# One ring of four PSUM bank pairs in place of three pairs and two single banks

## The chip, the cores and the metric

The kernel runs on one core of one Trainium2 chip. The metric is the device time of one execution in microseconds (us), the median of several executions. Five engines work side by side, each through its own list of instructions in order: TensorE (PE in the profile; its weight loads are PEld), VectorE (DVE), ScalarE (ACT), GpSimd (POOL) and SyncE (SP), which mainly starts DMA transfers. Matmuls write to PSUM; here it is used as eight banks of 512 fp32 values in each of 128 partitions. DVE and ACT read the results out of it, which is called evacuation below.

## The reference

The input `x` is 4 sequences of 1024 tokens with 256 channels. The program is two residual layers, both fp32:

```python
x = x + attention(layernorm(x))     # 16 heads of 16, causal, ALiBi bias, softmax, output projection
x = x + encoder(layernorm(x))
```

The encoder layer takes the *batch* axis (4 long) as its sequence: at each of the 1024 positions, the four tokens attend to each other with 16 heads. Its output is added and normalised to `h`. A router scores 8 experts for each token, and the larger index of the best two is taken. That expert computes `gelu(h @ w1.T + b1) @ w2.T + b2`; the result is added to `h` and normalised again.

## The kernel before

`fast_layer` computes everything; a second, general version stands behind a test at the end and does not run on these inputs.

**Attention.** A unit is 256 queries of one sequence (128 in the last quarter, for which two units per sequence are made). For each unit and each of four groups of four heads, a round takes up to 512 columns of keys times queries. `score` (L902) makes a round's scores for four heads in two tiles `sk` of two banks each; ACT turns each tile into `p` with one exponential (L910) that reads both banks at once; where the diagonal is crossed, POOL cuts it (L920). `weigh` (L950) multiplies two rounds' `p` with the values into one bank `pv`, and ACT copies it (L966) or DVE adds it (L968) to `yt`. The results go through DRAM to be arranged by channel, are divided by their sums (L1010), projected (L1022, tile `op`), and added to `x` by DVE (L1015).

**What stands between.** While attention runs, the layer norm, transposes and projections of later units (`xtp` L806, `qkp` L820, `vp` L841) and the first six of eight encoder fronts are worked in between the rounds. A front is 128 positions of all four sequences: norm, transposes (`utp`, L1512), projections to queries, keys and values (`qkvp`, L1533, evacuated by ACT at L1542 and by DVE at L1540), attention over the batch on DVE, transposes (`ctp`), output projection (`ao`, L1640, added into `u` by DVE at L1645), routing. A loop over pairs of rounds, `p`, writes down the order: scores of round `2p`, work for DVE and ACT (`E_slot`), work that uses TensorE (`D_slot`), scores of round `2p + 1`, and the weighted sums of the two rounds before. `E_slot` and `D_slot` fill up to fixed costs. The order is written out by hand, so no scheduler changes it; the program builder adds the waits between engines from who reads and writes each tile.

**Banks.** A pool hands out its tiles in turn: a new tile takes the place of the one that the pool handed out `bufs` tiles ago, and its first writer waits until the readers of that one are done. Before, scores have a pool `ps_s` of three tiles of two banks. Everything else that TensorE writes in this stage takes one bank from `ps_m`, which has two, through `bank`:

```python
def bank(name):
    n_banks[0] += 1
    return banks[n_banks[0] % len(banks)].tile([P, QC], F32, tag="m", name=name)
```

`banks` is `[ps_m, ps_m]`. When attention is over, a third bank, `ps_z`, joins the turn.

**Experts.** After attention come the last unit's projection, the last two fronts and 38 tiles of 128 tokens, gathered by expert (`mtp` L1790, `hid` L1806, `oe` L1825, results by L1852 to L1863). They have a pool of five banks of their own beside the three of `bank`.

Of the kernel before, what the change touches and what calls it, by code (L numbers as in the profile page):

```python
# [29 lines left out]
F32 = mybir.dt.float32  # L30
# [5 lines left out]
PSUM = bass.MemoryType.PSUM  # L36

P = 128
# [6 lines left out]
QC = 512  # L45
# [529 lines left out]
def fast_layer(ctx: ExitStack, tc: tile.TileContext, odd, x, wq, wk, wv, wp, w_in, w_out, w_r,  # L575
# [5 lines left out]
    pool = lambda name, bufs, **k: tc.tile_pool(name=name, bufs=bufs, **k)  # L581
# [3 lines left out]
    xpool = ctx.enter_context(pool("xpool", X_BUFS))  # L585
    fact = ctx.enter_context(pool("fact", 1))
    ends = ctx.enter_context(pool("ends", 1))
    ps_m = ctx.enter_context(pool("ps_m", 2, space=PSUM))
    ctx.enter_context(tc.manual_schedule())
    attention = ExitStack()  # L590
    pad = attention.enter_context(pool("pad", 1))
    act = attention.enter_context(pool("act", 1))
    probs = attention.enter_context(pool("probs", N_PROBS))
    ps_s = attention.enter_context(pool("ps_s", 3, space=PSUM))

    def const(name, shape, dtype=F32, into=keep):
        return into.tile(shape, dtype, tag=name, name=name)
# [4 lines left out]
        return t  # L602


    banks, n_banks = [ps_m, ps_m], [0]

    def bank(name):
        n_banks[0] += 1
        return banks[n_banks[0] % len(banks)].tile([P, QC], F32, tag="m", name=name)

    batches = [(c, b) for c in range(NC) for b in range(B)]

# [187 lines left out]
    def turn(n):  # L800
        xn = held.pop(("xn", n))
        xt = act.tile([P, CC, W], F32, tag="xt", name=f"xt_{n}", bufs=2)
        pm = bank(f"xtp_{n}")
        for cc in range(CC):
            for i in range(PC):
                nc.tensor.transpose(  # L806
                    pm[:, cc * W + i * P:cc * W + (i + 1) * P],
                    xn[:, i, cc * P:(cc + 1) * P], ident,
                )
        nc.scalar.copy(xt.rearrange("p c w -> p (c w)"), pm)  # L810
        held["xt", n] = xt

    def project_qk(n, half):

        c, b = batches[n]
        xt = held["xt", n]
        pm = bank(f"qkp_{n}_{half}")
        for k in range(2):
            for cc in range(CC):
                nc.tensor.matmul(  # L820
                    pm[:, k * W:(k + 1) * W], wqk[:, k, cc, half * P:(half + 1) * P],
                    xt[:, cc], start=cc == 0, stop=cc == CC - 1,
                )
        kq = act.tile([P, 2, W], F32, tag=f"kq{half}", name=f"kq_{n}_{half}", bufs=KQ_BUFS)
        nc.vector.tensor_copy(kq.rearrange("p k w -> p (k w)"), pm)  # L825
        rows_ = slice(half * P, (half + 1) * P)
        if c == 0:
            held["kq", n, half] = kq
            nc.sync.dma_start(k_of[b][rows_, :2 * W], kq.rearrange("p k w -> p (k w)"))
        else:  # L830
            own = k_of[b][rows_, :W]
            both = bass.AP(own.tensor, own.offset, [own.ap[0], ((c + 1) * W, 2), (1, W)])
            nc.sync.dma_start(both, kq)
# [41 lines left out]
    def blocks_of(u, r):  # L875

        n, i, size = units[u]
        first = batches[n][0] * PC + i
        some = QC // (size * P)
        return [  # L880
            (kb, max(0, kb - first) * P)
            for kb in range(some * r, min(some * (r + 1), first + size))
        ]

    def n_rounds(u):
        n, i, size = units[u]
        return -(-(batches[n][0] * PC + i + size) // (QC // (size * P)))

    def score(u, g, r):

        n, i, size = units[u]
        name = f"{u}_{g}_{r}"
        kt = slots[g][:, W:]
        qt = slots[g][:, i * P:(i + size) * P]
        own = r == n_rounds(u) - 1
        ps = [ps_s.tile([P, 2, QC], F32, tag="s", name=f"sk_{name}_{k}") for k in range(2)]
        width = 0
        for kb, off in blocks_of(u, r):
            to = width + size * P - off
            for h in range(4):  # L900
                rows_ = slice(h * S, (h + 1) * S)
                nc.tensor.matmul(  # L902
                    ps[h // 2][:, h % 2, width:to],
                    kt[rows_, kb * P:(kb + 1) * P], qt[rows_, off:], start=True, stop=True,
                )
            width = to
        pts = []
        for pair in range(2):
            pt = probs.tile([P, 2, QC], F32, tag="p", name=f"p_{name}_{pair}")
            nc.scalar.activation(  # L910
                pt[:, :, :width], ps[pair][:, :, :width], AF.Exp, scale=1.0 / math.sqrt(D)
            )
            pts.append(pt)
        if own:

            for pt in pts:
                blocks = pt.rearrange("p j (n q) -> p j n q", q=W)[:, :, :, 0:P]
                if size == 1:
                    blocks = pt[:, :, width - P:width].unsqueeze(2)
                nc.gpsimd.affine_select(  # L920
                    blocks, blocks, pattern=[[0, 2], [0, size], [1, P]],
                    compare_op=ALU.is_ge, fill=0.0, base=0, channel_multiplier=-1,
                )
        return pts

    def weigh(rounds_):

        parts = []  # L930
        for u, g, r, pts in rounds_:
            if not parts or parts[-1][0] != (u, g):
                parts.append(((u, g), []))
            parts[-1][1].append((r, pts))
        pm = bank("pv_{}_{}_{}".format(*rounds_[0][:3]))
        for k, ((u, g), of_part) in enumerate(parts):
            n, i, size = units[u]
            c, b = batches[n]
            vt = values[b % 2]
            pv = pm[:, k * W:k * W + size * P]  # L940
            blocks = [
                (kb, off, pts, first) for r, pts in of_part
                for first, (kb, off) in zip((True, False, False, False), blocks_of(u, r))
            ]
            for m, (kb, off, pts, first) in enumerate(blocks):
                at_p = 0 if first else at_p
                to = at_p + size * P - off
                for h in range(4):
                    at = (4 * g + h) * VD
                    nc.tensor.matmul(  # L950
                        pv[h * S:(h + 1) * S, off:], vt[:, kb, at:at + S],
                        pts[h // 2][:, h % 2, at_p:to],
                        start=m == 0, stop=m == len(blocks) - 1,
                    )
                at_p = to
        for k, ((u, g), of_part) in enumerate(parts):
            n, i, size = units[u]
            c = batches[n][0]
            pv = pm[:, k * W:k * W + size * P]
            if of_part[0][0] == 0 and g % 2 == 0:  # L960
                held["yt", g // 2] = ends.tile(
                    [P, 2, W], F32, tag="yt", name=f"yt_{u}_{g}", bufs=2
                )
            yt = held["yt", g // 2][:, :, :size * P]
            if of_part[0][0] == 0:
                nc.scalar.copy(yt[:, g % 2], pv)  # L966
            else:
                nc.vector.tensor_tensor(yt[:, g % 2], yt[:, g % 2], pv, ALU.add)  # L968
            if g % 2 and of_part[-1][0] == n_rounds(u) - 1:
                (nc.sync if c else nc.scalar).dma_start(  # L970
                    y_of[u][g - 1:g + 1].rearrange("g p w -> p g w"), yt
                )
# [1129 lines left out]
    def score_next(k):  # L2102
        u, g, r = rounds[k]
        waiting.append((u, g, r, score(u, g, r)))
        if r == n_rounds(u) - 1 and u < last_unit:
            to_fill.append((u + 1, g))
# [5 lines left out]
    for p in range(len(rounds) // 2):  # L2112
# [12 lines left out]
        fill()  # L2125
        E_slot(2 * p + 1, then)
    weigh(waiting)
    attention.close()


    for p in range(len(rounds) // 2, len(rounds) // 2 + 3):
# [11 lines left out]
    tail = ctx.enter_context(pool("tail", 1))  # L2143
    work = ctx.enter_context(pool("work", 2))
    ps_x = ctx.enter_context(pool("ps_x", 1, space=PSUM))
    banks.append(ctx.enter_context(pool("ps_z", 1, space=PSUM)))

    w1_sb, w2_sb = (const(name, [P, E - 1, CC, C], into=tail) for name in ("w1", "w2"))

# [50 lines left out]
    def begin(it):  # L2200
        if it.kind == "DQ" and ("qkv",) in held or it.kind[1:] == "C" and part.placed < NT - 1:
            return 1e9
        return max(it.ready, free[engine_of[it.kind[0]]])
# [26 lines left out]
    while threads:  # L2230
# [4 lines left out]
        at, _, it = min((begin(it) + FIRST_BY * n, n, it) for n, it in enumerate(threads))  # L2235
# [15 lines left out]
    while experts.left():  # L2251
# [4 lines left out]
        if n == 11:  # L2256
            pm = bank("n_badp")
# [4 lines left out]
@with_exitstack  # L2262
def tile_layer(ctx: ExitStack, tc: tile.TileContext, *args):
    nc = tc.nc
    flag = ctx.enter_context(tc.tile_pool(name="flag", bufs=1))
    odd = flag.tile([P, 1], I32, tag="odd", name="odd")
    fast_layer(tc, odd, *args)
    again = nc.values_load(
        odd[0:1, 0:1], min_val=0, max_val=1,
        skip_runtime_bounds_check_because="a comparison's result",  # L2270
    )
    with tc.If(again > 0):
        general_layer(tc, *args)
# [75 lines left out]
```

## Time and profile before

| | before |
|---|---|
| median of 3 executions | 857.03 us (854.6 to 857.36) |
| the profiled execution | 867.75 us |
| its span in the profile | 866.0 us |
| mean granted TensorE clock | 0.942 |
| busy: PE / PEld / DVE / ACT / POOL | 733.2 / 540.0 / 547.1 / 418.1 / 253.5 us |

The profile shows one execution, and a little slower one than the median; durations below are from it. A view of groups or of the timeline gives for each the engine, the line, what is written and read, and in square brackets how long the engine stood idle before it and what released it. A view of waits gives who waited for whom, the total, how often, and the longest. Busy time of PE is modelled at the ends of matmuls, which overlap. Line numbers in the text are those of the kernel before.

### The profile page before, as it was taken

The page shows a single profiled execution, that of the slowest core. Times are in us where ns is not written, and L with a number is a line of the kernel's source. Part 1 is how long each engine was busy: PE and PEld are TensorE (multiplying, and loading weights), DVE is VectorE, ACT ScalarE, POOL GpSimd, SP SyncE. Part 2 cuts the span into 40 slices and gives each one's busy share as a digit, 9 for nine tenths or more (in the row PEclk, how much of TensorE's full clock was granted, in tenths as well). Part 3 has the DMA queues.
Part 4 walks back from the last instruction along what each step waited for, and adds up shares of the span by engine and source line. Part 5 has one row for each costly group of instructions (what it writes and reads, how often), then busy time and mean ns, then how long its engine had stood idle before and what let it go on. Part 6 is the DMA issues. An engine that isn't in the chain of part 4 may idle for free. (4 is left out here: it accounts for less than half of the span.)

```text
span 866.0 us, 22430 instructions
## 1 busy us (share of the span) xinstructions
PE 733.2 (85%) x8917; PEld 540.0 (62%) x8917; DVE 547.1 (63%) x1316; ACT 418.1 (48%) x625; POOL 253.5 (29%) x360
## 2 busy tenths in 40 slices
PE   3898779998899789989989898897997699777892
PEld 2665557666565466655567666576776468666672
DVE  7245226429546947693678638469579669885663
ACT  1454436655455645564455447356655145333440
POOL 5443113212111312111122112022111323648875
PEclk9799979999999999999989999899998789998997
DMA  7345344433522414252444435235521572233430
GB/s 205 105 136 154 114 133 133 140 106 114 162 73 69 129 49 154 62 149 65 112 128 124 135 105 153 62 96 160 148 75 27 159 262 64 67 115 117 127 91 24
DMA packets 75219, 99.54 MB, mean 115 GB/s; under 512 B 19497, under 2 KB 58724, under 8 KB 74597
## 3 DMA queue, kind: packets, MB, share of 16 engines
q1 hardware_dynamic: 64576, 79.63, 31.3%
q0 software_dynamic: 4864, 14.16, 5.6%
q10 hardware_dynamic: 5668, 4.25, 1.6%
q8 instruction: 72, 1.18, 0.6%
q14 instruction: 39, 0.31, 0.1%
HBM read 61.55 MB, written 35.12 MB: 112 GB/s over the span
## 5 line engine op out<-in xcount | busy, mean ns | idle before, releaser
L910 ACT ACTIVATE p<-sk 128x1024 f32<-128x1024 f32 (+1 forms) x320 | 289.8, 938 | 183.5 <-PE sk L902 157.1
L920 POOL TENSOR_SCALAR_AFFINE_SELECT p<-p 128x512 f32<-128x512 f32 (+1 forms) x160 | 104.8, 659 | 476.7 <-ACT p L910 474.7
L902 PE MATMUL sk<-slots 32*128 32x128 f32 (+1 forms) x3456 | 188.5, 333 | 21.8 <-ACT p L910 13.6
L902 PEld LDWEIGHTS sk<-slots 32*128 32x128 f32 x3456 | 140.2, 192 | 71.5 <-issue 41.6
L950 PE MATMUL pv<-p,v 128*32 128x128 f32 (+1 forms) x3456 | 145.1, 316 | 9.6 <-DVE yn L1053 3.6
L950 PEld LDWEIGHTS pv<-p,v 128*32 128x32 f32 x3456 | 97.1, 112 | 47.0 <-issue 8.5
L1533 PE MATMUL qkvp<-w_in,ut 128*128 128x264 f32 (+1 forms) x256 | 99.1, 522 | 7.6 <-DVE x L1015 3.0
L1533 PEld LDWEIGHTS qkvp<-w_in,ut 128*128 128x128 f32 x256 | 45.9, 199 | 43.6 <-issue 26.4
L820 PE MATMUL qkp<-xt,wqk 128*128 128x256 f32 x256 | 66.4, 405 | 2.2 <-ACT xt L810 2.2
L1540 DVE COPY qkv<-qkvp 128x264 f32<-128x264 f32 x28 | 12.1, 433 | 77.5 <-PE qkvp L1533 77.5
L820 PEld LDWEIGHTS qkp<-xt,wqk 128*128 128x128 f32 x256 | 50.2, 202 | 13.2 <-ACT xt L810 2.6
L1825 PE MATMUL oe<-w,ge 128*128 (+1 forms) x152 | 42.7, 405 | 12.1 <-DVE mv_v L734 5.2
L1806 PE MATMUL hid<-mt,w 128*128 128x128 f32 x304 | 47.5, 294 | 6.0 <-DMA w<-in_w_dram 3.0
L1542 ACT COPY qkv<-qkvp 128x512 f32<-128x512 f32 (+1 forms) x36 | 20.2, 563 | 62.6 <-PE qkvp L1533 62.5
L825 DVE COPY kq<-qkp 128x512 f32<-128x512 f32 x32 | 21.9, 685 | 42.9 <-PE qkp L820 41.5
L1747 POOL DMA_INDIRECT given<-rows,rows x38 | 42.6, 1120 | 20.0 <-DVE at_t L1352 10.0
L1806 PEld LDWEIGHTS hid<-mt,w 128*128 128x128 f32 x304 | 42.0, 200 | 8.5 <-ACT ge L1815 3.3
L1022 PE MATMUL op<-wp,yc 128*128 128x256 f32 x124 | 35.0, 424 | 11.0 <-DVE yc L1010 11.0
L1863 POOL DMA_INDIRECT out_dram<-o,out_rows x38 | 39.4, 1036 | 8.7 <-issue 5.9
L1588 DVE TENSOR_TENSOR pv<-qkv,sc 128x1024 f32<-128x1024 f32 x32 | 39.7, 1239 | 0.1
L1567 DVE TENSOR_REDUCE sc<-pr 128x64 f32<-128x1024 f32 x32 | 39.0, 1220 | 1.1
L1566 DVE TENSOR_TENSOR pr<-qkv 128x1024 f32<-128x1024 f32 x32 | 39.4, 1232 | 0.0
(275 smaller groups left out, 994.6 us busy)
## 6 DMA issues: line engine op xcount, KB each, us to landing
slots<-k SPq DMA_DIRECT2D x128, 80.0 KB
k<-kq SPq DMA_DIRECT2D x32, 256.0 KB
v<-v SPq DMA_DIRECT2D x16, 288.0 KB
v<-v SPq DMA_DIRECT2D x4, 1152.0 KB
x<-in_x_dram SPq DMA_DIRECT2D x16, 256.0 KB
y<-yt SPq DMA_DIRECT2D x16, 256.0 KB
rows<-x SPq DMA_DIRECT2D x32, 128.0 KB
slots<-k SPq DMA_DIRECT2D x64, 64.0 KB
```

Source lines behind the costliest of these rows:

```text
L820: nc.tensor.matmul(pm[:, k * W:(k + 1) * W], wqk[:, k, cc, half * P:(half + 1) * P], xt[:, cc], start=cc == 0, stop=cc == CC - 1,)
L902: nc.tensor.matmul(ps[h // 2][:, h % 2, width:to], kt[rows_, kb * P:(kb + 1) * P], qt[rows_, off:], start=True, stop=True,)
L910: nc.scalar.activation(pt[:, :, :width], ps[pair][:, :, :width], AF.Exp, scale=1.0 / math.sqrt(D))
L920: nc.gpsimd.affine_select(blocks, blocks, pattern=[[0, 2], [0, size], [1, P]], compare_op=ALU.is_ge, fill=0.0, base=0, channel_multiplier=-1,)
L950: nc.tensor.matmul(pv[h * S:(h + 1) * S, off:], vt[:, kb, at:at + S], pts[h // 2][:, h % 2, at_p:to], start=m == 0, stop=m == len(blocks) - 1,
L1533: nc.tensor.matmul(pq, ut[:, cc, t * P:(t + 1) * P], w_in_sb[:, cc, lo:hi], start=cc == 0, stop=cc == CC - 1,)
L1566: nc.vector.tensor_tensor(pr, wide(qkv[:, t, 0:C]), qkv[:, :, C:2 * C], ALU.mult)
L1588: nc.vector.tensor_tensor(pr.rearrange("p s (h d) -> p s h d", d=D), qkv[:, :, 2 * C:3 * C].rearrange("p s (h d) -> p s h d", d=D), sc[:, ...
L1747: nc.gpsimd.indirect_dma_start(out=self.hx, out_offset=None, in_=t.rows_of, in_offset=bass.IndirectOffsetOnAxis(ap=t.rows_[:, self.j:self. ...
L1806: nc.tensor.matmul(ph[:, fc], self.w1[:, cc, fc * P:(fc + 1) * P], mt[:, cc], start=cc == 0, stop=False,)
L1825: nc.tensor.matmul(self.v, ge[:, fc], self.w2[:, fc] if self.w2 else late["w2"][:, bass.ds(at + fc * C, C)], start=fc == 0, stop=False,)
L1863: ins = nc.gpsimd.indirect_dma_start(out=out.rearrange("t n c -> (t n) c"), out_offset=bass.IndirectOffsetOnAxis(ap=t.table.out_rows[:, t. ...
```

## The change

`ps_m` goes, and `ps_s` gets a fourth pair, so that all eight banks are one ring of four pairs. Scores take a pair per tile, as they did. A weighted sum takes a pair and uses its first bank. Every other user asks `bank`, which gives the first half of a new pair and, to the next that asks, the second half; if a score or a weighted sum takes a pair in between, the second half is left unused. Pairs come in the order in which TensorE uses them. After attention the ring is closed, and a pool of three single banks serves `bank`, in place of two and one.

```diff
-    ps_m = ctx.enter_context(pool("ps_m", 2, space=PSUM))
...
-    ps_s = attention.enter_context(pool("ps_s", 3, space=PSUM))
+    ps_s = attention.enter_context(pool("ps_s", 4, space=PSUM))
...
-    banks, n_banks = [ps_m, ps_m], [0]
+    half_of = []
+    tail_banks = []
+
+    def pair_of_banks(name):
+        half_of.clear()
+        return ps_s.tile([P, 2, QC], F32, tag="s", name=name)
 
     def bank(name):
-        n_banks[0] += 1
-        return banks[n_banks[0] % len(banks)].tile([P, QC], F32, tag="m", name=name)
+        if tail_banks:
+            return tail_banks[0].tile([P, QC], F32, tag="m", name=name)
+        if half_of:
+            return half_of.pop()
+        pair = pair_of_banks(name)
+        half_of.append(pair[:, 1])
+        return pair[:, 0]
...
-        ps = [ps_s.tile([P, 2, QC], F32, tag="s", name=f"sk_{name}_{k}") for k in range(2)]
+        ps = [pair_of_banks(f"sk_{name}_{k}") for k in range(2)]
...
-        pm = bank("pv_{}_{}_{}".format(*rounds_[0][:3]))
+        pm = pair_of_banks("pv_{}_{}_{}".format(*rounds_[0][:3]))[:, 0]
...
     attention.close()
+    half_of.clear()
+    tail_banks.append(ctx.enter_context(pool("ps_m", 3, space=PSUM)))
...
-    banks.append(ctx.enter_context(pool("ps_z", 1, space=PSUM)))
```

## The prediction

> **What bounds the kernel now.** I read the page's totals and slices first, then a table of two stretches, then TensorE's waits, then single moments of the timeline. Totals and slices, from the page:
>
> ```profile
> PE 733.2 (85%) x8917; PEld 540.0 (62%) x8917; DVE 547.1 (63%) x1316; ACT 418.1 (48%) x625; POOL 253.5 (29%) x360
> ...
> PE   3898779998899789989989898897997699777892
> ...
> DVE  7245226429546947693678638469579669885663
> ```
>
> TensorE is the busy engine nearly everywhere. The attention stage, where the ring is used, ends near 690 us; the expert stage follows:
>
> ```profile
> 20.00:690.00 670.00, 590.83 (x8042) 423.13 (x8041) 409.42 (x918) 352.33 (x483) 141.77 (x205) 0.95 0.39 113
> 690.00:866.00 176.00, 135.25 (x854) 111.65 (x854) 122.31 (x350) 63.40 (x139) 100.11 (x131) 0.91 0.35 112
> ```
>
> The columns are length, then busy time of PE, weight loads, DVE, ACT and POOL, then granted clock and DMA. TensorE works 591 of 670 us, against 409 for DVE and 352 for ACT. So its order sets the time: what delays it by 1 us costs about 1 us, unless it soon stands still for another reason. The waits of TensorE in the first stretch (total, times, longest):
>
> ```profile
> PE sk L902 <- ACT p L910: 13.6, 17, 2.3
> PE op L1022 <- DVE yc L1010: 11.0, 6, 4.9
> ...
> PE turned_w L1433 <- DVE x L1015: 6.8, 1, 6.8
> ...
> PE qkvp L1533 <- DVE x L1015: 3.0, 2, 2.3
> PE pv L950 <- DVE x L1015: 2.6, 3, 1.7
> ```
>
> The first, third, fourth and fifth are waits for a bank: a score waits for the exponential that reads its pair, or a bank waits for its last reader. The second is a wait for data.
>
> **What the skill says.** The Trainium skill, "Perfetto Trace Analysis", section "Optimization Strategy", reads a gap that repeats on the saturated engine as a possible lack of PSUM. The trace agrees in part: bank waits are about 37 of 76 idle us between 20 and 690 us (summed below). Its section "Matmuls" asks for groups that rotate through different banks, so that an evacuation overlaps the next group. The kernel before does so; this is the timeline:
>
> ```profile
> 178.90 1.91 PE L1533 MATMUL qkvp<-w_in,ut 128*128 128x512 f32 x6
> ...
> 179.96 0.58 ACT L1542 COPY qkv<-qkvp 128x512 f32<-128x512 f32 x1 [1.70 <-PE qkvp L1533]
> ```
>
> The last four of these six matmuls go to the second bank, from 179.76 us; ACT starts to copy the first at 179.96. And "PSUM — Partial Sum Buffer", section "PSUM bank collisions raise a hardware error", asks for order between engines on one bank and quadrant, and reports different banks as clean. So the chip itself has no need of a wait between the halves of a pair.
>
> **The change, part by part.** Every engine's instructions keep their order and their number, DMA issues on the SP, ACT and POOL queues among them; only the waits differ (I compared the two built programs instruction by instruction; no time is in that). Nothing is moved past a queue.
>
> *1. Waits added inside a pair.* `bank` hands out two halves of one tile. In the built program the first matmul into the second half waits for the instruction that evacuates the first half, in 81 of 81 such pairs. Each half has its own bank, but the tile is followed as one. So I took, for each of the 81, the end of that evacuation in the profile of before, plus 0.1 us for the signal, less the start of the matmul that must now wait. For the copy above: 179.96 + 0.58 + 0.1 - 179.76 = 0.88 us, where before nothing was waited for. For the attention output:
>
> ```profile
> 236.78 1.10 PE L1640 MATMUL ao<-w_out,ct 128*128 128x264 f32 x4
> 236.98 0.43 DVE L1645 TENSOR_TENSOR u<-u,ao 128x264 f32<-128x264 f32 x1 [0.31 <-PE ao L1644]
> ```
>
> 236.98 + 0.43 + 0.1 - 236.78 = 0.73. Of the 81, 63 are such plain cases of 0.72 to 1.15 us, in sum **56.4 us**: the matmul was right behind, so all of it falls on TensorE. In 9 more the evacuation stands behind exponentials on ACT (1.4 to 2.4 us each), in sum **17.3**. In 9 it stands behind other DVE work (2.0 to 8.7 us), in sum **38.7**. The worst of these:
>
> ```profile
> 104.08 1.89 PE L820 MATMUL qkp<-xt,wqk 128*128 128x256 f32 x8
> ...
> 110.49 0.35 DVE L986 RECIPROCAL inverse<-sums 128x32 f32<-128x32 f32 x1 [8.30 <-DMA sums<-y]
> ...
> 111.98 0.68 DVE L1015 TENSOR_TENSOR x<-x,op 128x512 f32<-128x512 f32 x1
> ...
> 112.72 0.72 PEld L1433 LDWEIGHTS turned_w<-ident,w_out 128*128 128x128 f32 x4 [7.15 <-DVE x L1015]
> ```
>
> `op` takes the first half and `qkp` the second. DVE sits behind a reciprocal that waits for a DMA, so `qkp` would wait 8.7 us where before `turned_w` waited 6.8. Behind each waiting matmul stand the next scores, for which ACT waits, and then the weighted sums.
>
> *2. Waits added through the ring.* One order now serves scores, weighted sums and other banks, so an allocation waits for the fourth pair before it, whatever that was. Measured the same way, ten matmuls of scores and weighted sums find that pair late: **15.3 us**, the longest 3.1 (behind the sum of DVE at L1015) and twice 2.9 (behind L1719). All other allocations find it free.
>
> *3. Waits removed.* Gaps of TensorE over 0.15 us before a matmul whose wait for another engine is gone or replaced sum to 41.3 us. Two of them (2.7 and 1.6) are waits for data that another wait now covers, so **37.0** are gained, among them `turned_w` 6.8, `pv` for L1053 3.6, and 7.2 of the 13.6 at scores. What is late next is counted in 1 and 2.
>
> *4. The expert stage* had banks in turns of three (two and one); it has three again: nothing. The 176 us behind 690 move as a whole. A new pool opens over the released ring; the matmuls there carry no wait that a reader of the ring has not already met, so I take 0, with 3 us either way.
>
> *5. What absorbs.* A later TensorE meets other engines that are further on. Beyond the bank waits, 38 us of idle remain from 20 to 690 us, 23 of them behind DVE (L1010, L1627, L764 and the like); I take half, 11. Of the 53 us that stand behind backed-up DVE work (38.7 in 1 and 14 of the 15.3 in 2), a third, 17, since one or two short waits come between two such places and let DVE catch up about 1 us each. In sum 28; bounds 0, and 91 where both vanish wholly (38 + 53).
>
> *6. Clock.* The Trainium skill, "TensorE: Matmul & The Clock Gate", section "What's actually happening": after an idle window of about 3.4 us the array runs at half rate, and needs as long busy to recover. The trace agrees at the one long gap of before:
>
> ```profile
> 105.00:112.00 7.00, 0.97 (x5) 0.52 (x3) 1.41 (x7) 0.00 (x0) 0.00 (x0) 0.89 0.50 121
> 112.00:117.00 5.00, 4.28 (x36) 2.72 (x40) 2.98 (x11) 1.40 (x2) 1.25 (x2) 0.50 0.43 125
> ```
>
> The clock is 0.50 behind it. Six new waits are over 3.4 us; one of them replaces the gap above. An estimate from that page: half of 3.4, 1.7 us, for two of the other five, 3 us; bounds 0 and 9.
>
> Sum: 56.4 + 17.3 + 38.7 + 15.3 - 37.0 - 28 + 3 = **+66 us**. The profiled execution took 867.75 us, 866.0 of them its span, 1.2% over the median of 857.03; the sum would put it at 934. Applied to the median: **923 us**.
>
> **Rivals.** *More absorption.* DVE is busy only 409 of 670 us, so all its lags may vanish, and half of the remaining idle with them: 56.4 + 17.3 - 37.0 - 11, +26, gives 883. For it: DVE's slack. Against it: in the example above a DMA holds DVE, and a later TensorE does not help. *Nothing absorbed, and knock-on.* 127.7 - 37.0 is +91; with 9 us for the clock and some 10 us for allocations that found their pair free by under 1 us, +110: 948 to 967. For it: ACT and DVE take their work from TensorE, and move with it. *Faster.* The added waits fall where TensorE would have stood still anyway, and the 37 us remain. It decides once over 91 of the 127.7 us are absorbed, and all that step 5 could give is just that; it must also hide some of the plain waits, which no gap follows closely. With 3 in 10 of their 56 us hidden too, 17, it would be 840. *The change does not do what it says*, and the deeper ring makes no waits shorter: then 37 us are not gained, and +103 gives 960; but the program shows those waits gone.
>
> **How the numbers follow.** The sum of the parts 0.68; more absorption 0.12; knock-on, with the case of no gain, 0.16; faster 0.04. No change means within 0.3%, about what a measurement of this kernel can tell: only a place between the second and the last case, 0.02, taken from those two. Predicted 923. The range, 888 to 952, takes in absorption from 0 (+94) to 62 us (+32), and leaves out the worst knock-on and the lower part of the more-absorbed case. Faster 0.03, same 0.02, slower 0.95.
>
> **What would show it.** Right: new rows among TensorE's waits, each with 0.7 to 1 us a time: `qkvp` behind the copy at ACT (L1542 of before), `ao` behind DVE's sum into `u`, `xtp` and `qkp` behind the copy of `v`; the row of `turned_w` behind `x` gone, with `qkp` behind `x` in its place; TensorE's busy time the same and its share lower; the first stage some 65 us longer and the last still about 176. Wrong: if those rows are there, but the stage is longer by less than 30 us, step 5 is wrong; if `qkvp` starts its second bank while the first is copied, step 1 is.

## The result, and the profile after

The changed kernel takes **937.75 us** (median of 4, 932.87 to 940.25) against 856.49 us before: a ratio of 1.0945 with a 95% interval of 1.089 to 1.100, 81 us more. The forecast was 923 us within 888 to 952.

The page of the changed kernel, totals and slices. Its profiled execution took 932.87 us, the lowest of the four, with a span of 931.2. Its line numbers are 10 above those of before, and 11 in a few places near the end.

```profile
PE 748.2 (80%) x8917; PEld 540.4 (58%) x8917; DVE 546.0 (59%) x1316; ACT 418.7 (45%) x625; POOL 253.7 (27%) x360
...
PE   4886798987888799887877878788787679887983
```

Every engine has the same number of instructions as before, and DVE, ACT and POOL are busy for the same time within 1.1 us. TensorE is busy for 15 us longer (step 6 below), but its share is down from 85 to 80%, and sevens and eights fill the attention stage. The two stretches:

```profile
20.00:755.00 735.00, 605.71 (x8039) 422.33 (x8040) 404.49 (x907) 350.34 (x480) 139.68 (x203) 0.94 0.35 101
755.00:931.00 176.00, 136.22 (x859) 113.44 (x857) 126.00 (x359) 65.94 (x142) 102.60 (x133) 0.89 0.37 120
```

The expert stage still takes 176 us. All that was added lies in the first stretch, 735 us for 670. (The profiled execution of before was a long one; against a second profile of it, below, the attention stage grew by 75 us.) TensorE's waits there (total, times, longest):

```profile
PE op L830 <- DVE x L1025: 24.6, 8, 6.0
PE qkvp L1543 <- ACT qkv L1552: 15.7, 23, 0.8
...
PE vp L830 <- ACT v L856: 5.3, 5, 2.0
...
PE vp L816 <- ACT v L856: 4.1, 6, 0.7
...
PE ao L1650 <- DVE u L1655: 3.6, 7, 0.5
```

These are the rows that were forecast, with 0.5 to 0.7 us a time at `qkvp`, `ao` and `xtp` behind `v` in place of 0.7 to 1 (why, under the table of stalls). The tile's name is that of the pair's *first* user, the line that of the second: `op L830` is the query and key projection, written into the second half of the pair whose first half `op` holds, and waiting for `x` to be summed from it. One such place in the timeline:

```profile
196.85 1.02 PE L1543 MATMUL qkvp<-w_in,ut 128*128 128x512 f32 x2
...
197.91 0.59 ACT L1552 COPY qkv<-qkvp 128x512 f32<-128x512 f32 x1 [3.08 <-PE qkvp L1543]
198.55 0.74 PEld L1543 LDWEIGHTS qkvp<-w_in,ut 128*128 128x128 f32 x4 [1.50 <-ACT qkv L1552]
198.55 1.16 PE L1543 MATMUL qkvp<-w_in,ut 128*128 128x264 f32 x4 [0.68 <-ACT qkv L1552]
```

Before, the matmuls into the second bank began 0.2 us ahead of the copy of the first. Now they begin when it has ended. The longest wait of the forecast, at `op`:

```profile
107.56 0.35 DVE L996 RECIPROCAL inverse<-sums 128x32 f32<-128x32 f32 x1 [7.72 <-DMA sums<-y]
...
109.06 0.68 DVE L1025 TENSOR_TENSOR x<-x,op 128x512 f32<-128x512 f32 x1
...
109.80 1.22 PE L830 MATMUL op<-xt,wqk 128*128 128x256 f32 x2 [6.04 <-DVE x L1025]
```

DVE still waits for the DMA of the sums. TensorE now stands at `op`'s pair, with the projection not begun; before it stood one user later, with the projection done.

### The profile page after: what moved, and what is told of

It reads as the page before. It is cut to its first block, busy times and chain, and to the rows that moved or that the text cites. A ratio compares the mean times of both kernels' runs of the same rounds, so it can differ in the third digit from the quotient of the medians.

```text
span 931.2 us, 22522 instructions
## 1 busy us (share of the span) xinstructions
PE 748.2 (80%) x8917; PEld 540.4 (58%) x8917; DVE 546.0 (59%) x1316; ACT 418.7 (45%) x625; POOL 253.7 (27%) x360
## 5 line engine op out<-in xcount | busy, mean ns | idle before, releaser
L912 PE MATMUL sk<-slots 32*128 32x128 f32 (+1 forms) x3456 | 183.0, 335 | 14.0 <-DVE rank L1729 6.9
L960 PE MATMUL pv<-p,v 128*32 128x128 f32 (+1 forms) x3456 | 151.5, 325 | 7.2 <-DVE x L1025 3.0
L960 PEld LDWEIGHTS pv<-p,v 128*32 128x32 f32 x3456 | 101.3, 115 | 47.3 <-issue 11.5
L1543 PE MATMUL qkvp<-w_in,ut 128*128 128x264 f32 (+1 forms) x236 | 91.6, 506 | 15.7 <-ACT qkv L1552 15.7
L1543 PEld LDWEIGHTS qkvp<-w_in,ut 128*128 128x128 f32 x236 | 40.1, 193 | 54.2 <-ACT qkv L1552 35.5
L1552 ACT COPY qkv<-qkvp 128x512 f32<-128x512 f32 (+1 forms) x31 | 17.2, 559 | 62.9 <-PE qkvp L1543 62.8
L830 PE MATMUL op<-xt,wqk 128*128 128x256 f32 x64 | 24.2, 543 | 24.6 <-DVE x L1025 24.6
L1835 PEld LDWEIGHTS oe<-w,ge 128*128 128x128 f32 x152 | 27.3, 201 | 17.5 <-DVE given L1852 7.5
L1025 DVE TENSOR_TENSOR x<-x,op 128x512 f32<-128x512 f32 (+1 forms) x20 | 11.6, 578 | 42.1 <-PE op L1032 41.3
L830 PE MATMUL qkp<-xt,wqk 128*128 128x256 f32 x144 | 35.8, 391 | 0.2 <-ACT p L920 0.2
```

The source lines that it names most:

```text
L830: nc.tensor.matmul(pm[:, k * W:(k + 1) * W], wqk[:, k, cc, half * P:(half + 1) * P], xt[:, cc], start=cc == 0, stop=cc == CC - 1,)
L912: nc.tensor.matmul(ps[h // 2][:, h % 2, width:to], kt[rows_, kb * P:(kb + 1) * P], qt[rows_, off:], start=True, stop=True,)
L960: nc.tensor.matmul(pv[h * S:(h + 1) * S, off:], vt[:, kb, at:at + S], pts[h // 2][:, h % 2, at_p:to], start=m == 0, stop=m == len(blocks) - 1,
L1543: nc.tensor.matmul(pq, ut[:, cc, t * P:(t + 1) * P], w_in_sb[:, cc, lo:hi], start=cc == 0, stop=cc == CC - 1,)
L1835: nc.tensor.matmul(self.v, ge[:, fc], self.w2[:, fc] if self.w2 else late["w2"][:, bass.ds(at + fc * C, C)], start=fc == 0, stop=False,)
```

## The experiments

The theory: the second half of a shared pair waits for the reader of the first half, and that is what costs. The first rival: the common ring costs, since scores and weighted sums stand behind slow readers of other banks. Ratios are to the kernel before on the same chip, and "us" worked out from a ratio uses 857.

**All halves apart.** A loop ahead of `attention.close()` takes the order between two instructions of different engines out of the program, where one touches the first half and one the second of the same pair, and they share nothing else. The halves are different banks, so nothing is raced for. The heart of it, with the mark that each shared pair gets:

```diff
+    def halves_apart():
...
+                for other, was, w, r in shared[key]:
+                    if was != half and other.engine != ins.engine and not (w & rd or r & wr or w & wr):
+                        tc.declare_no_dep(ins, other, reason="two banks")
+                shared[key].append((ins, half, wr, rd))
...
+        shared[pair[:, 0].tensor.name] = []
...
+    halves_apart()
     attention.close()
```

> The changed kernel, with the order between the two halves of a pair taken out wherever the two instructions share no data: the second half's first matmul no longer waits for the reader of the first half (80 of 81 such waits go; in the last the matmul needs what that reader wrote). Ring, order and sharing stay. Theory (the waits inside a pair are the cost): the same count on the trace of before leaves 17 us of added waits against 33 us of removed ones, so about 841 us, 830 to 857, and TensorE's idle time in the attention stage falls from 132 us to 50 to 75. Rival (the common ring of four costs: scores and weighted sums stand behind slow readers of other banks): stays above 915 us. Rival (the slower clock and a later DVE cost, once set off): 870 to 900 us.

Measured: 835.34 us, ratio 0.9734 (0.9696 to 0.9771). That is 0.1211 below the changed kernel, 104 us, for waits counted at 110.7 us, and it beats the kernel before by 2.7%. TensorE's gaps in the stage sum to 55 us, as expected. The place of the prediction's first example in its timeline (line numbers 29 above those of before):

```profile
168.19 1.92 PE L1562 MATMUL qkvp<-w_in,ut 128*128 128x512 f32 x6
...
169.25 0.59 ACT L1571 COPY qkv<-qkvp 128x512 f32<-128x512 f32 x1 [1.19 <-PE qkvp L1562]
...
170.03 0.74 PEld L931 LDWEIGHTS sk<-slots 32*128 32x128 f32 x16 [0.34 <-ACT qkv L1571]
```

The six matmuls of both banks run through again, beside the copy. Of its waits, the longest in sum:

```profile
PE xtp L835 <- DVE xn L793: 14.7, 3, 8.3
PE ctp L1541 <- DVE ctx L1656: 8.8, 5, 2.5
PE sk L931 <- DVE rank L1748: 6.9, 2, 3.5
```

The first two are data. The third is what the ring adds, two waits of 3.5 us. So the ring of four does what it is for once its halves are independent. The rival falls, and so does the second one (870 to 900 us).

**A whole pair for each user**, so that nothing is shared and the ring turns faster:

```diff
-        if half_of:
-            return half_of.pop()
-        pair = pair_of_banks(name)
-        half_of.append(pair[:, 1])
-        return pair[:, 0]
+        return pair_of_banks(name)[:, 0]
```

> The changed kernel, but every user of a single bank takes a whole pair and leaves its second bank empty. No pair is shared, so no wait inside a pair; the ring turns faster (200 such pairs and weighted sums become 281). Theory: the count on the trace of before gives 27 us of added waits (25 of them at scores and weighted sums) against 28 us removed, so about 857 us, 845 to 872. Rival (turning the ring is the cost): slower than the changed kernel, above 938 us.

Measured: 847.89 us, ratio 0.9861 (0.9824 to 0.9898). That is within the 845 to 872 us expected. Even with a second bank thrown away at each use, the ring is 1.4% faster than the kernel before, and 93 us faster than the changed one. This run takes no order out by declaration, and says the same.

**Two pairs and four single banks**, the eight banks of before cut otherwise, without a common order:

```diff
-    ps_m = ctx.enter_context(pool("ps_m", 2, space=PSUM))
...
-    ps_s = attention.enter_context(pool("ps_s", 3, space=PSUM))
+    ps_s = attention.enter_context(pool("ps_s", 2, space=PSUM))
+    ps_m = attention.enter_context(pool("ps_m", 4, space=PSUM))
...
     attention.close()
+    banks[:] = [ctx.enter_context(pool("ps_n", 3, space=PSUM))]
```

> The kernel before, with two pairs for scores and four single banks, each a tile of its own, for everything else, in place of three pairs and two banks. It has the four spare banks of depth and no shared tile and no common order. Theory: the count on the trace of before gives 53 us of added waits at scores (82 of about 0.65 us, each for the exponential of the round before) against 40 removed, so some 865 us, 855 to 880. Rival (depth of banks outside scores decides): below 840 us.

Measured: 844.21 us, ratio 0.9835 (0.9798 to 0.9872); neither statement holds. Scores do wait more. TensorE's row for them, first from the second profile of the kernel before (next), then from this kernel (busy us, mean ns, idle us before):

```profile
L902 PE MATMUL sk<-slots 32*128 32x128 f32 (+1 forms) x3456 | 189.4, 334 | 18.1 <-ACT p L910 13.8 <-DMA slots<-kq 4.2
L902 PE MATMUL sk<-slots 32*128 32x128 f32 (+1 forms) x3456 | 215.4, 332 | 26.3 <-ACT p L910 23.0 <-DMA slots<-kq 2.3 <-DMA slots<-k 0.7
```

The gaps there are only 8 us longer, but the matmuls themselves fill 26 us more: the mean of one is the same, so those of the four heads overlap less. So some 34 of the 53 us counted are paid (40, where the starts of the same matmuls are compared at full clock), and a view of waits alone hides most of it. Against them, the gaps at all other matmuls of the stage fall by 39 us (40 were counted), and the time at half clock by 29 us (table below), which is worth up to 15 and was not in the forecast. In sum, with the 34, that is -20 us; the stage is 19 us shorter.

**The kernel before again**, for a second profile.

> The kernel before, unchanged, for a second profile of it: the first profiled execution took 867.75 us, 11 us over the median. If the profiled one was an odd execution, this one lies within 854 to 859 us and its attention stage ends near 673 us after the start of the span and not 683; if profiling itself costs, near 867 again.

Measured: 858.51 us, with a span of 856.7; the attention stage ends at 677 us, later than the 673 expected of an ordinary execution. The first profiled execution was an odd one by some 9 us, spread over start, attention and experts. The comparisons by stage below use this second profile.

**The same four banks as two shared pairs**, to have the wait alone, without a ring:

```diff
-    ps_m = attention.enter_context(pool("ps_m", 4, space=PSUM))
+    ps_m = attention.enter_context(pool("ps_m", 2, space=PSUM))
...
+        if n_banks[0] % 2:
+            half_of.append(ps_m.tile([P, 2, QC], F32, tag="m", name=name))
+            return half_of[0][:, 0]
+        return half_of.pop()[:, 1]
```

> The kernel of two score pairs and four single banks, with the four banks made as two tiles of two halves, handed out in the same turn. Against that kernel only the waits inside a pair differ; there is no common ring. 60 second halves find the reader of the first half late in the trace of before, in sum 65 us (52 of them under 1.2 us each). Theory (the wait inside a shared tile costs by itself): 844 + 65 less a tenth, about 903 us, 888 to 915. Rival (it costs only in the common ring, where scores stand behind it): within 10 us of 844.

Measured: 927.71 us, ratio 1.0780 (1.0743 to 1.0818), which is 81 us over the kernel with four single banks by the ratios. The direction settles it: the shared tile costs by itself. The size was off by 22 us, and outside the stated range; see the clock.

**Halves apart after `op` alone**, and **after `qkvp` alone**: the loop of the first experiment, for pairs whose first user has that name.

```diff
+        if name.startswith("op_"):
             shared[pair[:, 0].tensor.name] = []
```

> The changed kernel, with the order between halves taken out only in pairs whose first half is the attention's projection op (its reader is DVE's sum into x). 16 waits go, 35.7 us in the count on the trace of before, 26.2 of them in six waits of 2 to 9 us behind backed-up DVE work. If these long waits cost like the others (92% of the count, as in the kernel with all halves apart): 938 - 33, about 905 us. If a late DVE absorbs a third of them and more: 914 us or above. If the slow clock after a long stall adds to them: below 900 us.

Measured: 907.46 us, ratio 1.0560 (1.0524 to 1.0596): 33 us below the changed kernel, for 35.7 counted.

> The changed kernel, with the order between halves taken out only in pairs whose first half is qkvp (its reader is a copy on ACT). 23 waits go, each of 0.88 to 0.98 us, 20.6 us in the count. If a short wait falls on TensorE in full: 938 - 20, about 917 us. If short waits are half hidden: about 928 us.

Measured: 918.12 us, ratio 1.0682 (1.0646 to 1.0718): 23 us below, for 20.6 counted. Each of the two differences is uncertain by some 6 us either way, so both agree with the count, and short waits that are half hidden (10 us) are excluded. A third given back on the long waits after `op` would have left 27 us of the 33, at the edge of the interval; the profile of the changed kernel adds that the six of them, counted at 26.2 us, stand there with gaps of 24.4. So little or nothing was given back.

**Halves kept across scores**, on top of all halves apart:

```diff
-        half_of.clear()
         return ps_s.tile([P, 2, QC], F32, tag="s", name=name)
...
-        pm = pair_of_banks("pv_{}_{}_{}".format(*rounds_[0][:3]))[:, 0]
+        pm = bank("pv_{}_{}_{}".format(*rounds_[0][:3]))
```

> The kernel with all halves apart (835 us), where besides a weighted sum takes a half like any other user and an open second half is kept for the next user when a score comes in between: 140 second halves in place of 81, so the ring turns more slowly. The count on the trace of before gives 16 us of added waits for 17 and 36 removed for 37: no change, 828 to 842 us. If the ring's turn (scores behind DVE's rank and x, 10 us) is what is left to gain: 826 us or below.

Measured: 839.86 us, ratio 0.9762 (0.9717 to 0.9808); the same as all halves apart within the intervals. No gain from a slower turn of the ring is seen.

**Stalls and clock by kernel.** Worked out from the records of the profiles, from the start of the first matmul of scores to the start of the last unit's projection: its length, TensorE's gaps over 0.15 us, the rest, and how long the granted clock was one half.

| kernel | stage | gaps | rest | half clock |
|---|---|---|---|---|
| before, again | 655.4 | 68.8 | 586.7 | 61.0 |
| changed | 730.9 | 127.9 | 602.8 | 87.5 |
| all halves apart | 629.5 | 54.8 | 574.5 | 51.0 |
| apart after `op` | 702.1 | 105.2 | 596.6 | 78.5 |
| apart after `qkvp` | 712.4 | 112.4 | 599.8 | 92.0 |
| two pairs, four singles | 636.0 | 37.7 | 598.4 | 31.8 |
| two pairs, two shared | 723.9 | 94.9 | 629.2 | 85.7 |

A stall costs more than its gap. The kernels run the same matmuls in the same order, so each can be compared with itself, from its start to the next one's start. Of the 81 places of step 1, 79 lie in this stage; there the changed kernel takes 103.6 us longer than the kernel with all halves apart, and 102.5 longer than the second profile of before. The gaps at these places sum to only 90.3 us: matmuls in sequence overlap by about 0.16 us in the records, and one that waits loses that. With the 23 waits after `qkvp` gone, the gaps fall by 15.5 and the rest by 3.0 us while the half clock does not fall.

What remains of the growth of the "rest" goes with the clock. Matmuls at half clock that had no wait before them are in sum 22.7 us over the same matmuls at full clock (the median of the three fastest of the ten profiles) in the second profile of before, and 32.2 in the changed kernel. (The two kernels with two score pairs can be compared in their "rest" with each other only, for the 26 us of scores above.) A stretch of the changed kernel, in the columns of the tables above:

```profile
152.00:156.30 4.30, 4.25 (x69) 2.79 (x68) 2.02 (x7) 3.01 (x5) 1.88 (x3) 1.00 0.23 87
156.30:159.90 3.60, 1.67 (x24) 1.30 (x28) 0.91 (x2) 1.91 (x4) 0.00 (x0) 1.00 0.41 114
159.90:163.30 3.40, 3.40 (x40) 1.88 (x36) 1.12 (x4) 1.96 (x3) 1.42 (x2) 0.50 0.20 67
```

A wait of 1.98 us at 156.3 (the transposes behind ACT's copy of the first half) is followed by 3.4 us at half clock. Between the two kernels with four banks outside scores, the shared pairs have 54 us more at half clock, and their matmuls there, without a wait before them, take 21 us longer: about the 22 us by which that forecast was short. The clock was not tried by itself: no kernel here holds the waits and keeps the clock.

## Why the prediction was right, and by how much

**Step 1** was right in cause and size. It counted 112.4 us. In the stage, 79 of the 81 places take 102.5 us more from start to start than in the second profile before, and taking 80 of the waits away gives 104 us of the 110.7 counted for those. About half of the difference is the signal: the step took 0.1 us for it, and in the profile after it is 0.05.

**Step 2** counted 15.3 us for ten matmuls; their gaps sum to 14.3, the two at `rank` longer (3.5 each), one gone.

**Step 3** was right: with the waits of step 1 away, 17 added and 33 to 37 removed leave 16 to 20 us of gain, and that kernel is 23 us below the kernel before. The deeper ring gains; the sharing loses more than four times that.

**Step 4**: the last matmul follows the end of attention by 163.4 us in the changed kernel and by 163.6 in the second profile before. Nothing, as said.

**Step 5** took 28 us of absorption. The stage grew by 75.5 us, 9.5 of them for the clock (next); the rest, 66, is 25 below the 90.7 counted net. That the size held is in part luck, since its split was not right: the long waits behind DVE were to give back a third, and the six after `op` cost 25.3 of the 26.2 us counted, from start to start. What shrank were in part gaps for other reasons: those before the attention's projection, 12.4 us in the second profile of before, are 3.3 after, and those of scores behind the DMA of `slots` went from 4.2 us to none.

**Step 6 is the term that was mis-sized**: 3 us, as two of five long waits at 1.7 us. In the stage after, nine stretches at half clock follow a wait of over 3.4 us, with 53 us in sum; in the second profile before three do, with 17. So it was not two but all of the new long waits that set the clock back, and for 5.9 us on average, which is worth up to 3 us and not 1.7. Stretches behind shorter waits became fewer, seven with 34 us for eleven with 44. Together the half-clock time grew from 61.0 to 87.5 us, and the matmuls in it by 9.5 us, at the step's upper bound of 9. With that and the lost overlap TensorE's busy time rose, where the prediction had said that it stays the same. So the stage grew by 75 us and not by 66. The profiled execution after is also 5 us below its median, which is most of the way from 75 to 81.

**The rivals.** More absorption (883) kept the short waits and needed all long ones behind DVE to vanish; the kernel apart after `op` shows that they don't. The faster case (840) needed short waits to hide as well; the kernel apart after `qkvp` shows that they don't. Knock-on with nothing absorbed (948 to 967) had the clock right and the absorption wrong. That the ring shortens no waits (960) is refuted by all halves apart.

## What to carry to other kernels

A tile that spans two banks is followed as one when its halves go to different users: look in the program's waits for a second half that waits for the first half's reader, before counting on depth. Give each independent user a tile of its own, even at the price of an empty bank: here a whole pair for each was 93 us faster than sharing. And price a new wait on the busiest engine in the profile of before, as the end of what it waits for less the start of what must wait: for the waits inside a pair that count held within a tenth, of that for scores in two pairs a quarter to a third was not paid. For an engine behind a clock that falls on idling, add to it. To measure such a wait afterwards, compare the starts of the same instructions; gaps alone show too little.

## What the runs showed of the hardware that was not expected

The Trainium skill, "TensorE: Matmul & The Clock Gate", section "What's actually happening", gives about 3.4 us of idling as what halves the clock. The traces agree above that: in the stage of the ten profiles, all 39 gaps of over 3.4 us that began at full clock were followed by half clock, within 3.4 us of their end at the latest. But below it the clock fell too: so after 24 of 26 gaps of 2.6 to 3.4 us, after 44 of 63 of 1.9 to 2.6, and after 23 of 84 of 1.0 to 1.9 (some of these had other gaps near them). Stretches lasted 3.4, 6.8 or 10.2 us. A sum of waits of 2 us each is then dearer than it looks.

This stood in the trace that the prediction read. It named one long gap, of four over 3.4 us in the stage, but eight of the 13 stretches at half clock in the stage before follow gaps of at most 2.3 us. One of them, after a single gap of 2.29 us that ended at 494.8:

```profile
492.50:496.10 3.60, 1.31 (x5) 0.70 (x5) 2.65 (x9) 0.00 (x0) 0.00 (x0) 1.00 0.88 215
496.10:499.50 3.40, 3.40 (x10) 1.60 (x12) 0.16 (x1) 0.59 (x1) 0.00 (x0) 0.50 0.88 303
```

What share of which stretch must be idle is not settled by these runs: another of the eight, at 124.1 us, follows a gap of 0.24 us alone, behind matmuls of eight columns.
